# Softmax denominators of a causal latent attention: added over key blocks on VectorE, then summed by one set of products per chunk of heads

## The chip, the cores and the metric

The kernel runs on one core of one Trainium2 chip. The metric is device time in microseconds (us) of one execution. The kernel before took 2323.1 us in the median of three runs (2315.94 to 2333.15).

Names used below: PE is TensorE (matrix products), PEld its weight loads, DVE is VectorE, ACT is ScalarE, POOL is GpSimd, SP is the engine that issues most transfers.

## The reference, cut to what matters

The kernel computes a network of two layers on `x` of shape (2, 1024, 128): latent attention, a spiking feed-forward, a state-space block, linear attention, head attention and mixtures of experts. The change touches only the first block, for batch 0:

```python
q = einsum('bld,dhk->blhk', x_bld, Wq)
latent = einsum('bld,dc->blc', x_bld, Wkv_down)
k = einsum('blc,chk->blhk', latent, Wk_up)
v = einsum('blc,chk->blhk', latent, Wv_up)
attn = einsum('bqhd,bkhd->bhqk', q, k) / sqrt(64)
attn = softmax(where(causal mask, attn, -big), axis=-1)
y = einsum('bhqk,bkhd->bqhd', attn, v)
out = einsum('bqhd,hdo->bqo', y, Wout)
```

There are 16 heads, 1024 queries and keys, and a latent of 32 numbers. All is float32, but for the small bfloat16 operands named below.

## The kernel before, in words

`LatentAttention` folds the key weights into the queries, so that a score is a product over the 32 latent numbers, and uses the latent itself as the values. The 16 heads are four chunks `c` of four heads `j`. The four heads of a chunk lie in the four groups of 32 partitions.

`attend(b, ...)` does one batch, in two halves of 512 queries. Half 0 has 4 key blocks of 128 keys, half 1 has 8. A unit of work is one pair (chunk, key block), so half 0 has 16 units and half 1 has 32. In a unit `exponentials` (L282 to L301) does:

- L282: four float32 products, one for each head, that give the scores with keys on partitions. Each takes 32 rows of the array and all 128 columns. The shapes in the profile read 32\*128.
- L291: four bfloat16 products that add the negative row maximum of each query. They use the same 32 rows.
- L301: two ACT instructions that take the exponential of two heads each, from the PSUM tile `a0_st` (3 buffers of two heads) to the SBUF tile `a0_pT` (6 buffers of two heads).
- L304: on a diagonal block, where keys and queries meet, POOL sets what the causal mask forbids to zero, 128x256 elements for each pair of heads. All 4 blocks of half 0 and the last 4 of half 1 are diagonal. On these the width falls from 512 queries to 384, 256 and 128.

Then `weigh` (L320 to L336) does, one unit later:

- L320: four products of the exponentials with the latent, one for each head. Each takes all 128 rows and 32 columns of the array (128\*32 in the profile). They accumulate over the key blocks in the PSUM tile `a0_oT`, which has one buffer.
- L328: four products of the same exponentials with columns of ones, into the PSUM tile `a0_dT`. They accumulate the denominators over all chunks and key blocks of the half. Also 128\*32.
- L336: after the last key block of a chunk, DVE copies `a0_oT` to `a0_oU`.

The steps run one unit ahead: the scores of unit k+1 are issued ahead of the weighing of unit k. At the end of a half DVE takes the reciprocal of `a0_dT` (L348), PE spreads it over the heads (L352), DVE multiplies (L353), PE applies the output weights (L358) and DVE adds to the residual (L362).

Batch 0 runs by itself (`drain(latent.attend(0, ...))`, L1217), and a list scheduler decides the order of instructions on each engine there. Batch 1 runs in an order written by hand: `weave(space[0].loop(work, bank), attend, 1.75)` takes 1.75 steps of `attend(1)` for each step of the state-space loop (L637 to L639: two products and one scan on DVE for each step), then drains the rest. A step is what lies between two `yield`s.

In the profile a float32 product counts twice, since it is done in two passes: four products are x8. A bfloat16 product counts once. A short name such as `a_pT` stands for `a0_pT`.

Of the kernel before, what the change touches and what calls it, by code (L numbers as in the profile page):

```python
# [9 lines left out]
F32 = mybir.dt.float32  # L10
# [9 lines left out]
P = 128  # L20
# [67 lines left out]
def drain(steps):  # L88
    for _ in steps:
        pass  # L90
# [20 lines left out]
class LatentAttention:  # L111
# [3 lines left out]
    C, J, LD = 4, 4, 32  # L115
# [146 lines left out]
        nc.vector.tensor_copy(self.nmT[b], pt.rearrange("p a b -> p (a b)"))  # L262
        yield

    def attend(self, b, work, ps, ps_o):
        g, nc, C, J = self.g, self.g.nc, self.C, self.J
        qT, latT, lat, nmT = self.qT[b], self.latT[b], self.lat[b], self.nmT[b]
        for half in range(2):
            kbs = list(range(4 * half + 4))
            dT = ps_o.tile([P, 512], F32, name="a0_dT")  # L270
            oU = work.tile([P, C, 512], F32, name="a0_oU")
            oTs = {}

            def exponentials(c, kb):

                off = max(kb * P - half * 512, 0)
                q0 = half * 512 + off
                n = 512 - off
                ss = [ps.tile([P, 2, 512], F32, name="a0_st") for _ in range(2)]
                for j in range(J):  # L280
                    quad = slice(32 * j, 32 * j + 32)
                    nc.tensor.matmul(  # L282
                        ss[j // 2][:, j % 2, off:],
                        latT[quad, bass.ts(kb, P)],
                        qT[quad, c, q0 : q0 + n],
                        start=True,
                        stop=False,
                    )
                for j in range(J):
                    quad = slice(32 * j, 32 * j + 32)  # L290
                    nc.tensor.matmul(  # L291
                        ss[j // 2][:, j % 2, off:],
                        self.addm[quad, c, :],
                        nmT[quad, q0 : q0 + n],
                        start=False,
                        stop=True,
                    )
                pTs = []
                for s in ss:
                    pT = work.tile([P, 2, 512], F32, name="a0_pT", bufs=6)  # L300
                    nc.scalar.activation(pT[:, :, off:], s[:, :, off:], AF.Exp)  # L301
                    if kb * P >= half * 512:
                        diag = pT[:, :, off : off + P]
                        nc.gpsimd.affine_select(  # L304
                            out=diag,
                            in_=diag,
                            pattern=[[0, 2], [1, P]],
                            compare_op=ALU.is_ge,
                            fill=0.0,
                            base=0,  # L310
                            channel_multiplier=-1,
                        )
                    pTs.append(pT)
                return pTs, off

            def weigh(c, kb, pTs, off):
                if kb == 0:
                    oTs[c] = ps_o.tile([P, 512], F32, name="a0_oT")
                for j in range(J):
                    nc.tensor.matmul(  # L320
                        oTs[c][32 * j : 32 * j + 32, off:],
                        lat[:, kb, :],
                        pTs[j // 2][:, j % 2, off:],
                        start=(kb == 0),
                        stop=(kb == kbs[-1]),
                    )
                for j in range(J):
                    nc.tensor.matmul(  # L328
                        dT[32 * j : 32 * j + 32, off:],
                        self.ones[:, c, :],  # L330
                        pTs[j // 2][:, j % 2, off:],
                        start=(c == 0 and kb == 0),
                        stop=(c == C - 1 and kb == kbs[-1]),
                    )
                if kb == kbs[-1]:
                    nc.vector.tensor_copy(oU[:, c, :], oTs.pop(c))  # L336

            units = [(c, kb) for c in range(C) for kb in kbs]
            held = {}
            for step in range(len(units) + 1):  # L340
                if step < len(units):
                    held[step] = exponentials(*units[step])
                if step >= 1:
                    weigh(*units[step - 1], *held.pop(step - 1))
                yield

            rec = work.tile([P, 512], F32, name="a0_rec")
            nc.vector.reciprocal(rec, dT)  # L348
            yield
            for c in range(C):  # L350
                rr = ps.tile([P, 2, 512], F32, name="a0_st")
                nc.tensor.matmul(rr[:, 0, :], self.pick[:, c, :], rec, start=True, stop=True)  # L352
                nc.vector.tensor_mul(oU[:, c, :], oU[:, c, :], rr[:, 0, :])  # L353
            yield
            for i in range(4):
                pf = ps.tile([P, 2, 512], F32, name="a0_st")
                for c in range(C):
                    nc.tensor.matmul(  # L358
                        pf[:, 0, :D], oU[:, c, bass.ts(i, P)], self.wvo[:, c, :], start=(c == 0), stop=(c == C - 1)
                    )  # L360
                xt = g.x[:, b * TPB + 4 * half + i, :]
                nc.vector.tensor_add(xt, xt, pf[:, 0, :D])  # L362
            yield
# [832 lines left out]
def first_layer(g, w, open_experts, load_expert):  # L1196
# [3 lines left out]
    def pool(stack, name, bufs, **kw):  # L1200
        return stack.enter_context(tc.tile_pool(name=name, bufs=bufs, **kw))
# [7 lines left out]
    latent = LatentAttention(g, w, pool(latents, "a0_keep", 1, **right))  # L1209
    own = pool(latents, "a0_batch1", 1, **right)  # L1210
    with ExitStack() as es:
        latent.project([pool(es, "a0_batch0", 1), own])
        with tc.tile_pool(name="a0_seq", bufs=1) as seq, tc.tile_pool(name="a0_ps_a", bufs=2, space=PSUM) as ps:
            drain(latent.row_maxima(0, seq, ps, 4))
        work = pool(es, "a0_work", 2)
        ps, ps_o = pool(es, "a0_ps_b", 3, space=PSUM), pool(es, "a0_ps_o", 1, space=PSUM)
        drain(latent.attend(0, work, ps, ps_o))  # L1217

    bank = banks(spaces, "bank", 2)
    shared = StateConstants(g, w, pool(spaces, "s_one", 1))  # L1220
# [25 lines left out]
    with tc.manual_schedule(engines=ALL):  # L1246
        with (
            tc.tile_pool(name="a0_seq", bufs=1, **right) as aseq,
            tc.tile_pool(name="a0_ps_a", bufs=3, space=PSUM, **right) as ps,
        ):  # L1250
            maxima = latent.row_maxima(1, aseq, ps, 2)
            weave(into_space(0, bank), maxima, 1.25)
            drain(maxima)
        work = pool(latents, "a0_work", 1, **right)
        ps, ps_o = pool(latents, "a0_ps_b", 2, space=PSUM, **right), pool(latents, "a0_ps_o", 1, space=PSUM, **right)
        attend = latent.attend(1, work, ps, ps_o)
        with tc.tile_pool(name="s_work", bufs=1, reuse_waits="tile") as work:
            weave(space[0].loop(work, bank), attend, 1.75)
        drain(attend)
        latents.close()  # L1260
        open_experts()
        with ExitStack() as es:
            bank0, bank1 = banks(es, "bank0", 3, **right), banks(es, "bank1", 3, **right)
            side = into_space(1, bank1, **right)
            weave(out_of_space(0, bank0, load_experts()), side, 1.2)
            drain(side)
        ework = pool(ends, "e_work", 2, **right)
        ps_e, ps_o = pool(ends, "e_ps", 2, space=PSUM, **right), pool(ends, "e_ps_o", 1, space=PSUM, **right)
        experts = expert_steps(g, w, [0, 1], ework, ps_e, ps_o)
        with tc.tile_pool(name="s_work", bufs=1, reuse_waits="tile") as work:  # L1270
            weave(space[1].loop(work, bank), experts, 1.4)
        spaces.close()
        with ends, ExitStack() as es:
            weave(out_of_space(1, banks(es, "bank", 3)), experts, 0.6)
            drain(experts)
# [3 lines left out]
def kernel(ctx: ExitStack, tc: tile.TileContext, d: dict, out: bass.AP):  # L1279
# [30 lines left out]
    def load_expert(e):  # L1310
        for name in ("Wg", "Wu"):
            nc.sync.dma_start(out=w[name][:, e, :], in_=d[name][e])
        nc.sync.dma_start(out=w["Wd"][:, e], in_=d["Wd"][e].rearrange("(c p) o -> p c o", p=P))

    first_layer(g, w, open_experts, load_expert)
    layer0.close()
    experts_ffn(g, w, [2])
# [70 lines left out]
```

## Time and profile before

| what | value |
|---|---|
| median of three runs | 2323.1 us |
| the profiled execution: its time / its span | 2328.53 us / 2326.8 us |
| products of batch 0, half 0 (147.87 to 198.51 us) | 50.64 us |
| its end: reciprocal to the next scores | 12.30 us |
| products of batch 0, half 1 (210.81 to 305.49 us) | 94.68 us |
| its end | 14.04 us |
| PE busy / DVE busy / ACT busy in the products of half 1 | 92.72 / 3.63 / 53.50 us |
| state-space loop with batch 1 (486.9 to 703 us) | 216.10 us |
| PE busy / DVE busy over the whole span | 87% / 70% |

The stages lie one after the other on the time axis of the trace. A busy PE in this profile is not a PE at its peak: a product that fills a quarter of the array counts as busy just as one that fills it.

The order of the built program can be listed engine by engine. On PE it is the order in which the trace shows the products, with one freedom that the prediction describes.

### The profile page before, as it was taken

What the parts mean: (1) busy time and instruction counts of PE and PEld (TensorE: products, weight loads), DVE (VectorE), ACT (ScalarE), POOL (GpSimd) and SP (SyncE); (2) the same over time, 40 slices, a digit from 0 to 9 for tenths busy, and PEclk for the clock granted to TensorE, in tenths of its full rate; (3) what the DMA queues carried; (4) which work ended last, traced back from release to release, by engine and by line L of the source; (5) the groups of instructions that cost most, each with busy time, mean ns of one, the idle gap of its engine ahead of it and who ended that gap; (6) DMA issues with size and microseconds to landing.
All of it is one profiled execution on the core that took longest, in us unless ns stands there. A gap on an engine that the chain in (4) does not pass through costs nothing. (4 is left out here: it accounts for less than half of the span.)

```text
span 2326.8 us, 36810 instructions
## 1 busy us (share of the span) xinstructions
PE 2015.9 (87%) x15152; PEld 1184.5 (51%) x15152; DVE 1629.0 (70%) x1988; ACT 1183.5 (51%) x1486; POOL 854.9 (37%) x460
## 2 busy tenths in 40 slices
PE   7779988887987748789698799999977999999999
PEld 4323344323334313235345577677755777777754
DVE  5851047788974659993423699899978999999732
ACT  1014521353643458764322576777735777777632
POOL 0001100033320000000102277878788787877700
PEclk9789997878998879899799899999989999999999
DMA  3000000076732067640000266566556665665500
GB/s 86 1 1 1 2 1 1 18 190 152 185 93 89 4 159 184 162 106 0 1 1 0 64 153 157 145 152 157 146 150 152 157 155 155 153 162 146 137 5 5
DMA packets 72647, 220.19 MB, mean 95 GB/s; under 512 B 9056, under 2 KB 19744, under 8 KB 72352
## 3 DMA queue, kind: packets, MB, share of 16 engines
q1 hardware_dynamic: 53584, 149.40, 21.5%
q0 software_dynamic: 18432, 67.12, 15.3%
q8 instruction: 119, 1.95, 0.3%
q10 hardware_dynamic: 464, 1.33, 0.3%
q14 instruction: 48, 0.39, 0.1%
HBM read 78.35 MB, written 5.24 MB: 36 GB/s over the span
## 5 line engine op out<-in xcount | busy, mean ns | idle before, releaser
L1075 POOL TENSOR_TENSOR h_a<-h_e,h_r 128x2048 f32<-128x2048 f32 x128 | 581.4, 4542 | 130.4 <-PE h_po L1081 93.9
L1041 DVE TENSOR_REDUCE h_m<-h_s 128x128 f32<-128x2048 f32 x128 | 293.2, 2291 | 73.2 <-PE h_s L1030 73.1
L1065 PE MATMUL h_pd<-h_e,ident 128*128 128x128 f32 x2048 | 267.4, 285 | 43.4 <-DMA h_e<-h_e 29.6
L1050 ACT ACTIVATE h_e<-h_e 128x1024 f32<-128x1024 f32 x256 | 256.5, 1049 | 89.6 <-DVE h_e L1047 71.4
L1047 DVE TENSOR_TENSOR h_e<-h_s,h_m 128x2048 f32<-128x2048 f32 x128 | 292.6, 2286 | 3.4 <-DVE h_m L1041 1.7
L1065 PEld LDWEIGHTS h_pd<-h_e,ident 128*128 128x128 f32 x2048 | 244.6, 196 | 87.3 <-DVE x_res L914 41.5
L304 POOL TENSOR_SCALAR_AFFINE_SELECT a_pT<-a_pT 128x256 f32<-128x256 f32 x128 | 97.2, 775 | 431.4 <-ACT a_pT L301 430.5
L301 ACT ACTIVATE a_pT<-a_st 128x1024 f32<-128x1024 f32 (+1 forms) x192 | 145.1, 808 | 139.1 <-PE a_st L291 137.0
L886 ACT ACT_TABLE_LOAD x105 | 134.7, 1283 | 150.5 <-PE e_pgu L879 150.3
L806 DVE TENSOR_TENSOR e_h<-e_sg,e_pu 128x512 f32<-128x512 f32 x128 | 87.0, 686 | 176.5 <-PE e_pu L802 151.2
L243 DVE TENSOR_REDUCE a_nm<-a_s 128x2 f32<-128x1024 f32 (+7 forms) x144 | 168.4, 1218 | 48.5 <-PE a_s L234 24.2
L804 ACT ACTIVATE e_sg<-e_pg 128x512 f32<-128x512 f32 x128 | 76.0, 596 | 192.5 <-PE e_pg L801 192.3
L825 PE MATMUL e_po<-e_h,Wd 128*128 128x512 f32 x256 | 139.4, 630 | 39.4 <-DVE e_h L806 39.3
L225 PE MATMUL a_s<-a_latT,a_qT 32*128 32x512 f32 (+3 forms) x768 | 128.7, 650 | 49.4 <-DVE a_nm L243 47.6
L905 PEld LDWEIGHTS h_pd<-Wd,e_h 128*128 128x128 f32 x1024 | 125.5, 191 | 90.1 <-DVE e_h L894 76.8
L1030 PE MATMUL h_s<-h_qz,h_kT 32*128 32x512 f32 x1024 | 148.5, 649 | 19.5 <-DVE h_e L1047 13.9
L879 PE MATMUL e_pgu<-e_uT,Wg 128*128 128x256 f32 x512 | 154.1, 383 | 4.0 <-ACT h_qz L994 2.1
L905 PE MATMUL h_pd<-Wd,e_h 128*128 128x128 f32 x1024 | 149.1, 287 | 5.9 <-DVE e_h L894 3.7
L879 PE MATMUL e_pgu<-e_uT,Wu 128*128 128x256 f32 x512 | 152.3, 379 | 0.0
L1060 POOL DMA_DIRECT2D h_e<-h_e x128 | 113.6, 887 | 104.0 <-DVE h_m L1041 48.8
L638 DVE TENSOR_TENSOR_SCAN s_h<-s_a,s_h 128x1024 f32<-128x1024 f32 x64 | 147.4, 2303 | 5.9 <-ACT s_a L606 1.7
L801 PE MATMUL e_pg<-e_uT,Wg 128*128 128x512 f32 x256 | 141.9, 638 | 2.1 <-ACT e_uT L794 2.1
(246 smaller groups left out, 3191.6 us busy)
## 6 DMA issues: line engine op xcount, KB each, us to landing
h_e<-h_e SPq DMA_DIRECT2D x128, 512.0 KB, 4.0
h_e<-h_e POOLq DMA_DIRECT2D x128, 512.0 KB, 4.6
s_a<-s_steps SPq DMA_DIRECT2D x64, 512.0 KB, 4.8
s_h<-s_steps SPq DMA_DIRECT2D x64, 512.0 KB, 6.3
s_steps<-s_delta SPq DMA_DIRECT2D x4, 512.0 KB, 2.6
s_steps<-s_dtx SPq DMA_DIRECT2D x4, 512.0 KB, 3.4
Wg<-in_Wg_dram SPq DMA_DIRECT2D x8, 256.0 KB, 6.0
Wu<-in_Wu_dram SPq DMA_DIRECT2D x8, 256.0 KB, 5.9
```

The lines of the kernel that those rows point to most:

```text
L243: nc.vector.tensor_reduce(nm[:, half, i, h : h + together], s[:, :, :n], AX.X, ALU.max, negate=True)
L301: nc.scalar.activation(pT[:, :, off:], s[:, :, off:], AF.Exp)
L638: nc.vector.tensor_tensor_scan(h, a, h, 0.0, ALU.mult, ALU.add)
L801: nc.tensor.matmul(pg, w["Wg"][:, e, f], opened[n], start=True, stop=True)
L879: nc.tensor.matmul(pgu[:, k, :], w[name][:, e, f], uT, start=True, stop=True)
L905: nc.tensor.matmul(po[:, t, :], h[:, bass.ts(t, P)], self.w["Wd"][:, e, fc, :], start=(k == 0), stop=(k == 1))
L1030: nc.tensor.matmul(s[:, j, :].rearrange("p (k q) -> p k q", k=K), kTs[b][quad, bass.ts(kb, P)], qzs[b][quad, :, bass.ts(qb, P)], start=Tru ...
L1041: nc.vector.tensor_reduce(m, heads.rearrange("p h q -> p q h"), AX.X, ALU.max)
L1047: nc.vector.tensor_sub(e, heads, m.unsqueeze(1).to_broadcast([P, H, P]))
L1050: nc.scalar.activation(eh, eh, AF.Exp, scale=scale)
L1065: nc.tensor.matmul(pd, g.ident, e2[:, k, :], start=(k == 0), stop=(k == 7))
L1075: nc.gpsimd.tensor_mul(a, e, r.unsqueeze(1).to_broadcast([P, H, P]))
```

## The change

For batch 0 alone (`added=True`):

- The exponentials of key block 0 of a chunk go to two new tiles, `a0_sum0` and `a0_sum1` (two buffers each), in place of `a0_pT`.
- The products with ones are no longer issued for each unit. For every key block after the first, DVE adds the exponentials to the sum tiles, two instructions for each unit (L347 of the changed kernel).
- One set of four products with ones for each chunk (L324 of the changed kernel) sums the tiles over the keys. It is issued one step after the weighing of the chunk's last block.
- The loop over steps has one step more, for both batches: `range(len(units) + 2)`. For batch 1 the added step holds no work, but it is a `yield`, so that `attend(1)` has 64 of them in place of 62.

```diff
-    def attend(self, b, work, ps, ps_o):
+    def attend(self, b, work, ps, ps_o, added=False):
...
-                for s in ss:
-                    pT = work.tile([P, 2, 512], F32, name="a0_pT", bufs=6)
+                for k, s in enumerate(ss):
+                    if added and kb == 0:
+                        pT = work.tile([P, 2, 512], F32, name=f"a0_sum{k}")
+                        total[c, k] = pT
+                    else:
+                        pT = work.tile([P, 2, 512], F32, name="a0_pT", bufs=6)
...
+            def denominators(c, pTs, off, first, last):
+                for j in range(J):
+                    nc.tensor.matmul(
+                        dT[32 * j : 32 * j + 32, off:],
+                        self.ones[:, c, :],
+                        pTs[j // 2][:, j % 2, off:],
+                        start=first,
+                        stop=last,
+                    )
...
-                for j in range(J):
-                    nc.tensor.matmul(
-                        dT[32 * j : 32 * j + 32, off:],
-                        self.ones[:, c, :],
-                        pTs[j // 2][:, j % 2, off:],
-                        start=(c == 0 and kb == 0),
-                        stop=(c == C - 1 and kb == kbs[-1]),
-                    )
+                if not added:
+                    denominators(c, pTs, off, c == 0 and kb == 0, c == C - 1 and kb == kbs[-1])
+                elif kb > 0:
+                    for k, pT in enumerate(pTs):
+                        nc.vector.tensor_add(total[c, k][:, :, off:], total[c, k][:, :, off:], pT[:, :, off:])
...
-            for step in range(len(units) + 1):
+            for step in range(len(units) + 2):
                 if step < len(units):
                     held[step] = exponentials(*units[step])
-                if step >= 1:
+                if 1 <= step <= len(units):
                     weigh(*units[step - 1], *held.pop(step - 1))
+                if added and step >= 2 and units[step - 2][1] == kbs[-1]:
+                    c = units[step - 2][0]
+                    denominators(c, [total.pop((c, k)) for k in range(2)], 0, c == 0, c == C - 1)
                 yield
...
-        drain(latent.attend(0, work, ps, ps_o))
+        drain(latent.attend(0, work, ps, ps_o, added=True))
```

The scheduler of batch 0 then builds another order on PE. Below is that order for half 0, from the weighing of block 1 of the second chunk to that of the third chunk, in both programs. S is scores (L282), M the row maximum (L291), W weighing (L320), D ones (L328), with the width behind the letter; a and b are the two pairs of heads, 1 and 2 a single head of pair a; a bar stands where PE goes from products of the 32\*128 shape to the 128\*32 shape or back.

```
before: W384ab D384ab | S128ab M | W256ab D256ab | S512a M S512b M | W128ab D128ab | S384ab M |
        D512a | S256a | W512ab D512b | M S256b M | W384ab ...
after:  W384a | S128(1) | W384b | S128(2) M S128b M | W256a | S512(1) | W256b | S512(2) M S512b M |
        W128a | S384(1) | W128b | S384(2) M | D512a | S384b M | D512b | S256a M | W512ab | S256b M | W384a ...
```

And one chunk of half 1, from the weighing of its block 1 to that of the next chunk:

```
before: W512ab D512ab | S512 M | W512ab D512ab | S512 M | W512ab D512ab | S384 M | W512ab D512ab | S256 M |
        W384ab D384ab | S128 M | W256ab D256ab | S512 M | W128ab D128ab | S512 M | D512ab | S512(1) |
        W512ab | S512(2) M S512b M | W512ab ...
after:  W512ab | S512 M | W512ab | S512 M | W512ab | S384 M | W512a | S256(1) | W512b | S256(2) M S256b M |
        W384ab | S128 M | W256a | S512(1) | W256b | S512(2) M S512b M | W128a | S512(1) | W128b |
        S512(2) M | D512a | S512b M | D512b | S512a | W512ab | S512b M | W512ab ...
```

More of the change, by code (lines that the diff above doesn't have):

```diff
@@ L271, in attend @@
             oU = work.tile([P, C, 512], F32, name="a0_oU")
-            oTs = {}
+            oTs, total = {}, {}
             def exponentials(c, kb):
```

## The prediction

> **What bounds the kernel now.** I read the stages in the windows view first, because the change touches only the attention of batch 0, then the timeline of one unit, then a unit whose groups are broken, then the waits.
>
> ```profile
> core 0: us, PE busy (x) PEld busy (x) DVE busy (x) ACT busy (x) POOL busy (x), PEclk, DMA share, GB/s
> 147.87:198.51 50.64, 49.01 (x448) 18.15 (x448) 2.68 (x5) 23.43 (x34) 12.81 (x32) 0.93 0.01 1
> 210.81:305.49 94.68, 92.72 (x897) 29.13 (x896) 3.63 (x9) 53.50 (x67) 13.51 (x33) 0.98 0.01 1
> ```
>
> In both product stages PE is busy almost throughout, ACT about half of the time, DVE hardly at all. So PE bounds them, and what PE sheds could count. How much a product is worth has to be read from starts:
>
> ```profile
> 222.56 1.15 PE L282 MATMUL a_st<-a_qT,a_latT 32*128 32x512 f32 x8
> 223.52 0.40 PE L291 MATMUL a_st<-a_nmT,a_addm 32*128 32x512 bf16 x4
> 223.85 1.06 PE L320 MATMUL a_oT<-a_pT,a_lat 128*32 128x512 f32 x8
> 224.00 1.94 ACT L301 ACTIVATE a_pT<-a_st 128x1024 f32<-128x1024 f32 x2 [1.20 <-PE a_st L291]
> 224.73 1.04 PE L328 MATMUL a_dT<-a_pT,a_ones 128*32 128x512 f32 x8
> 225.70 1.14 PE L282 MATMUL a_st<-a_qT,a_latT 32*128 32x512 f32 x8
> ```
>
> Four products of one kind, one for each head, run side by side and take one slot: 0.96 us for the scores, 0.33 for the row maximum, 0.88 for the weighing, 0.97 for the products with ones with the turn back to scores. The next rows show what a slot costs that is not full:
>
> ```profile
> 179.60 1.05 PE L328 MATMUL a_dT<-a_pT,a_ones 128*32 128x512 f32 x4
> 180.58 0.70 PE L282 MATMUL a_st<-a_qT,a_latT 32*128 32x256 f32 x4
> 181.21 1.06 PE L320 MATMUL a_oT<-a_pT,a_lat 128*32 128x512 f32 x8
> ...
> 240.20 1.12 PE L282 MATMUL a_st<-a_qT,a_latT 32*128 32x512 f32 x2
> 241.25 1.06 PE L320 MATMUL a_oT<-a_pT,a_lat 128*32 128x512 f32 x8
> 242.25 0.69 PE L282 MATMUL a_st<-a_qT,a_latT 32*128 32x512 f32 x1
> ```
>
> One head's score (x2) takes 1.05 us to the next start, two heads' ones (x4) 0.98: as much as four. And the two shapes do not overlap. So the price is set by how often PE changes between 32\*128 and 128\*32, not by how many products there are. From such rows I take, for widths 512, 384, 256 and 128: scores 0.965, 0.75, 0.54, 0.32; row maximum 0.325, 0.27, 0.22, 0.17; weighing or ones 0.89, 0.67, 0.46, 0.24; 0.09 more where PE turns from 128\*32 to 32\*128, or back straight from scores. (Groups of a and b that stand in one stretch between two bars count once.)
>
> ```profile
> DVE a_oU L336 <- PE a_oT L320: 138.9, 8, 25.7
> L637 DVE TENSOR_TENSOR s_h<-s_h,s_Bx x64: 1161/1219/1425, 486.9 to 1035.7; 128x1024 f32<-128x1024 f32 x64
> L304 POOL TENSOR_SCALAR_AFFINE_SELECT a_pT<-a_pT x128: 401/407/2387, 152.8 to 674.3; 128x256 f32<-128x256 f32 x128
> ```
>
> The first row, of the waits of 150 to 345 us, says that DVE sat idle 138.9 us waiting for PE: room for the added work. The second prices an addition of the new kind, both operands in SBUF. The third is for the contention below.
>
> **Part by part.**
>
> *Products with ones.* 192 products become 32: 160 leave, which looks like 40 slots. By the rebuilt order it is otherwise. Taken out, they leave the weighing waiting for ACT or POOL, and the scheduler fills that with the next scores, one head at a time. Stretches of one shape rise from 108 to 156 (half 0 40 to 68, half 1 68 to 94).
>
> Half 0, one chunk in the order that the change lists. Before, ten stretches: 1.43 + 0.49 + 1.01 + 1.29 + 0.57 + 1.02 + 0.98 + 0.63 + 1.87 + 0.76 = 10.05 us; the trace has 10.66 for it (173.15 to 183.81), the rest being a wait for ACT. After, 18 stretches by row of the list: W384a to S128b M 0.76 + 0.41 + 0.76 + 0.49 = 2.41; W256a to S512b M 0.55 + 1.06 + 0.55 + 1.29 = 3.43 (rounded parts); W128a to S384(2) M 0.33 + 0.84 + 0.33 + 1.02 = 2.51; D512a to S256a M 0.98 + 1.02 + 0.98 + 0.76 = 3.73; W512ab and S256b M 1.74. Sum 13.8 us: 3.1 us more, with fewer products.
>
> Half 1, one chunk. Before: 2 x (1.865 + 1.29) + 2.885 + 2.625 + 1.915 + 2.295 + 1.855 + 4.295 = 22.18 us; trace 22.83 (220.70 to 243.53). After: 2 x 2.27 + 2.00 + 3.34 + 1.25 + 3.43 + 3.00 + 4.30 + 2.27 = 24.1 us. Here 0.89 us is saved in each of the three units that stay whole, and more is lost in five broken places.
>
> Summed over the whole order, half 0 goes from 43.0 to 50.2 us, half 1 from 87.5 to 89.9.
>
> *Waits.* In a whole unit of half 1, ACT takes 2 x 1.0 us and the period falls to 2.27, so pair b's weighing waits for ACT where ones used to stand: I take 2.39 (from 224.00 + 1.94 to the next), 0.12 for each of three. On the diagonal 0.7 a chunk for selects that DVE stretches (next item). So 24.1 + 0.4 + 0.7 = 25.2 us a chunk. Half 0 keeps its start waits, less one cold D512.
>
> *Additions on DVE.* 80 instructions. Width 2x512 1.22 us (L637), 2x256 0.69 (the copies of 128x512), 2x384 between them, 0.95 as an estimate; 2x128 0.42, between 0.29 (L362, 128x128) and 0.69. Half 0: 8 x (0.95 + 0.69 + 0.42) = 16.5 us; half 1: 8 x (4 x 1.22 + 0.95 + 0.69 + 0.42) = 55.5. All beside PE: 72 of the 138.9 idle us. A whole unit wants 2.45 us of DVE against 2.39 of PE, a lag that block 0 (no addition) repays: 14 us of DVE a chunk against 25. Queued behind an addition is only the copy L336, which frees `a0_oT`; between the last weighing of a chunk and the first of the next stand two ones stretches and two score stretches, 3.7 us, against 0.42 x 2 + 0.69. Cost 0; without that cover, at most 0.84 x 8 = 7 us.
>
> *Selects on POOL.* 32 diagonal units, 0.41 us each alone. Next to DVE instructions with two SBUF inputs (batch 1 runs beside L637 and L639) they stretch: the mean of the 128 is 775 ns, so batch 1's 64 average 2 x 0.775 − 0.41 = 1.14, up to 2.39. Bounds here: 0 to 1 us for each unit. I take 0 in half 0, where a one-head score stretch stands between a select and its weighing, and the 0.7 above in half 1; these are the nearest, since DVE is busy a third to a half of the time here.
>
> *Ends of the halves.* The last set of ones waits for DVE's last addition and takes 0.98 in place of 0.24: +1.5 in half 0, +0.4 in half 1 where more of it is covered. Half 0: start −2.0 (the first W384 at 160.47 before, at about 158.5 after, one cold D512 less), nothing for the first chunk (12.7 by its stretches, 12.68 in the trace), 3.14 for each of the next two, tail +1.5: reciprocal at about 204.4 against 198.51, +5.9 (rounded). By sums, 50.2 + 4.85 start waits + 1.6 tail = 56.6 against 50.64, the same. Half 1: start −0.8, three chunks x (25.2 − 22.83) = +7.0, tail +0.4: +6.6.
>
> *ACT and memory.* ACT does the same exponentials, into other tiles; the two buffers of each sum tile come free a chunk ahead. DMA: SP's order is unchanged, nothing is queued past anything. Cost 0.
>
> *The added step of batch 1.* `attend(1)` has 64 yields in place of 62, of which the 35 steps of the loop take 61.25. In the middle PE, with 1.75 x 3.3 us of units a step, stays the slower one beside DVE's 4.8 us a step: 0 (bounds −2 and +2). At its end the order on DVE changes: the scan of the last step (679.12 to 683.9 in the trace, between reciprocal and L353) now stands before the reciprocal, and its results feed PE while DVE is at the residual. From 675.25 to the last L664 the trace has 27.7 us; with the reordered rows I get 24.0: −3.7 (bounds −6 and +1).
>
> Sum: +5.9 + 6.6 − 3.7 = **+8.8 us** on the profiled 2328.53, 2337. That run lies 5.4 above the median of three, so 2332 against 2323.1: +0.4%. What a measurement here can tell from no change is about 1%.
>
> *A rule against the trace.* The four scores start within 0.03 us of each other at 222.56 although the built order of many units is S of pair a, M of a, S of b, M of b, and M starts at 223.52 only: later instructions pass an earlier one that waits. The Trainium skill, "TensorE: Matmul & The Clock Gate", Part 3 ("Packing small matmuls"), has matmuls strictly in program order. By it each unit with M ahead of S b would pay a second score slot; such units rise from 30 to 44 of 48, 8.4 us more, and the sum would be +17. The measured starts decide; the sum above does not use the rule.
>
> **Rivals.**
>
> 1. *The removed products are paid in full* (faster). It needs broken groups to overlap with the other shape. A chunk then loses its ones slots, less one set of 0.98: 2.26 − 0.98 in half 0, 5.82 − 0.98 in half 1, four each: −24.5 us, and with −3.7 at the end of batch 1, 2295. Against it: 240.20 to 241.25, one head alone at full price.
> 2. *Selects or additions hold PE* (slower). If each of the 32 diagonal units waited as long as batch 1's selects stretch at the typical worst, 1.38 against 0.41, it is +31 on top: 2363. It takes over 1% from about 14 such units on. For it: 2.39 us seen. Against: DVE here is far less busy than with batch 1.
> 3. *The granted clock falls* (slower), because PE's half-filled stretches count as less: 0.98 in half 1 against 0.86 and 0.76 in the ends of the halves. some 100 us of half 1 at 0.81 (the mean of those two) in place of 0.98 are about +20: 2352. For it: half 0 stands at 0.93 with its waits. Against: PE does not pause more.
> 4. *The broken groups cost nothing* because waits for ACT in the old order go at the same time: only the end of batch 1 and small gains remain, about −4: 2319.
>
> **How the numbers follow.** Forecast 0.73 (its own range 2321 to 2344: −2 to +21 on the median, from the bounds of selects, the batch-1 end and the split chunks); rival 1 0.05, rival 2 0.12, rival 3 0.04, rival 4 0.06. Faster by over 1% is rival 1, 0.05. Slower by over 1% (above 2346) is rivals 2 and 3 and 0.03 of the forecast's upper end, 0.19; the rest 0.76. The range 2312 to 2353 takes in rivals 3 and 4 and leaves out 1 and 2, 0.17, and a little at the edges.
>
> **What would show it.** Product stages of about 56.5 and 101 us; middle chunks of 13.8 and 25.2 us between the same weighings; one-head and two-head stretches at full price; additions of 1.22 us beside PE, no wait of PE on DVE but at the ends; L304 near 0.41 in half 0 and stretched in half 1; a clock still at 0.93 and 0.98; the end of the loop some 4 us earlier against its start. Wrong if a one-head stretch is cheaper than 1 us beside the other shape, if PE waits for POOL by more than 1 us a chunk, or if the clock falls.

## The result, and the profile after

The changed kernel took 2340.4 us in the median of 20 executions (2325.0 to 2375.1), the kernel before 2322.1 (2312.0 to 2334.6, also 20). The ratio is 1.0062, with a 95% interval of 1.0040 to 1.0084: about 14 us slower, 0.6%. Ratios, here and below, leave out executions over 1.5% above the fastest of their kernel, here the four longest of the 20 (2361 and up); the medians keep them, and by the medians the change is 18 us slower. The forecast was 2332, and +8.8 us.

The profiled execution took 2328.1 us, with a span of 2326.4: as long as that of the kernel before (2326.8). So the first lesson is that this one pair of profiles does not show the loss. The windows view of the changed kernel, same columns as before:

```profile
core 0: us, PE busy (x) PEld busy (x) DVE busy (x) ACT busy (x) POOL busy (x), PEclk, DMA share, GB/s
142.56:198.18 55.62, 53.62 (x352) 17.65 (x352) 19.52 (x29) 23.68 (x34) 14.77 (x32) 0.97 0.00 1
211.73:308.48 96.75, 93.80 (x673) 27.52 (x672) 59.90 (x66) 53.84 (x67) 22.57 (x33) 1.00 0.00 1
```

Half 0 now has 352 records of products in place of 448, and half 1 has 673 in place of 897. Yet they take 55.6 us (+5.0) and 96.75 us (+2.1). PE is busy throughout as before. DVE has gone from 2.7 and 3.6 us to 19.5 and 59.9.

| stage (profiled pair) | before | after | difference |
|---|---|---|---|
| up to the first score of batch 0 (untouched) | 147.87 | 142.56 | −5.3 |
| products of half 0 | 50.64 | 55.62 | +5.0 |
| reciprocal to next scores | 12.30 | 13.55 | +1.3 |
| products of half 1 | 94.68 | 96.75 | +2.1 |
| its end | 14.04 | 13.44 | −0.6 |
| state-space loop with batch 1, start of the first scan (the instruction behind the first L637) to the end of batch 1's last addition to the residual | 214.74 | 209.32 | −5.4 |
| all that follows, and the stage ahead of the scan | | | +2.6 |

The sum is −0.4. The first line goes with a clock difference in a stage that both kernels share: 0.86 before (0 to 147.87 us) and 0.93 after (0 to 142.56 us), with PE busy 104.0 and 96.8 us.

The timeline of the changed kernel, first a whole unit of half 1, then a broken group of half 0:

```profile
222.45 1.15 PE L284 MATMUL a_st<-a_qT,a_latT 32*128 32x512 f32 x8
223.41 0.40 PE L293 MATMUL a_st<-a_nmT,a_addm 32*128 32x512 bf16 x4
223.75 1.06 PE L336 MATMUL a_oT<-a_pT,a_lat 128*32 128x512 f32 x8
224.74 1.09 PE L284 MATMUL a_st<-a_qT,a_latT 32*128 32x384 f32 x8
...
167.09 0.63 PE L336 MATMUL a_oT<-a_pT,a_lat 128*32 128x256 f32 x4
167.65 1.12 PE L284 MATMUL a_st<-a_qT,a_latT 32*128 32x512 f32 x2
168.70 0.63 PE L336 MATMUL a_oT<-a_pT,a_lat 128*32 128x256 f32 x4
```

A stretch is what PE does between two changes of shape; a thin one holds products of one or two heads in place of four. From 222.45 to 224.74 a unit without ones takes 2.29 us, where the kernel before needed 3.14 (222.56 to 225.70). But at 167.65 one head's score takes 1.05 us to the next start, between two weighings of two heads each. Such places ate the saving.

The waits of 150 to 350 us and two rows by line:

```profile
DVE a_sum L347 <- PE a_oT L336: 45.3, 8, 7.2
DVE a_oU L349 <- PE a_oT L336: 19.5, 8, 3.2
```

```profile
L347 DVE TENSOR_TENSOR a_sum<-a_sum,a_pT x80: 409/958/1476, 149.7 to 306.5; 128x1024 f32<-128x1024 f32 x32, 128x768 f32<-128x768 f32 x16, 128x512 f32<-128x512 f32 x16, 128x256 f32<-128x256 f32 x16
```

```profile
L310 POOL TENSOR_SCALAR_AFFINE_SELECT a_pT<-a_pT x120: 401/710/2387, 149.1 to 676.8; 128x256 f32<-128x256 f32 x120
```

DVE still waits for PE for 65 us, so it is not the bound. The 80 additions lie between 0.41 and 1.48 us, by width. The median of the selects rose from 407 to 710 ns. That row has batch 1's in it, which were stretched before; of batch 0's, the 32 of half 0 took 14.77 us in all, 0.46 each, and the 32 of half 1 21.87 us, 0.68 each, where each had taken 0.41.

### The profile page after: what moved, and what is told of

Read it like the earlier page. It is cut to its first block, busy times and chain, and to the rows that moved or that the text cites. A ratio compares the mean times of both kernels' runs of the same rounds, so it can differ in the third digit from the quotient of the medians.

```text
span 2326.4 us, 36321 instructions
## 1 busy us (share of the span) xinstructions
PE 2011.6 (86%) x14832; PEld 1173.1 (50%) x14832; DVE 1701.8 (73%) x2068; ACT 1183.8 (51%) x1486; POOL 866.5 (37%) x460
## 3 DMA queue, kind: packets, MB, share of 16 engines
q1 hardware_dynamic: 53584, 149.40, 21.6%
## 5 line engine op out<-in xcount | busy, mean ns | idle before, releaser
L310 POOL TENSOR_SCALAR_AFFINE_SELECT a_pT<-a_pT 128x256 f32<-128x256 f32 x120 | 104.8, 892 | 314.4 <-ACT a_pT L307 313.7
L307 ACT ACTIVATE a_pT<-a_st 128x1024 f32<-128x1024 f32 (+3 forms) x176 | 130.4, 789 | 124.2 <-PE a_st L293 122.0
L225 PE MATMUL a_s<-a_latT,a_qT 32*128 32x512 f32 (+3 forms) x768 | 122.9, 615 | 51.0 <-DVE a_nm L243 49.3
L654 DVE TENSOR_TENSOR_SCAN s_h<-s_a,s_h 128x1024 f32<-128x1024 f32 x64 | 147.0, 2297 | 5.5 <-ACT s_a L622 1.2
```

The lines of the kernel that those rows point to most:

```text
L654: nc.vector.tensor_tensor_scan(h, a, h, 0.0, ALU.mult, ALU.add)
```

## The experiments

The theories. **Groups**: the scheduler's new order breaks the groups of four heads, and thin stretches cost as much as whole ones. **Contention**: DVE's additions stretch the selects on POOL, and PE waits. **Clock**: the thin order changes what clock PE is granted. In all tables, ratios are to the kernel before on the same chip, with 95% intervals.

### The changed kernel again, three profiles in all

No edit: a second series of 12 executions, then one single execution more, each with a profile.

> The changed kernel once more, nothing edited, to see what of its time belongs to the stages and what to the granted clock. Theory (broken groups of four heads): the products of half 0 take 55.6 us again and those of half 1 96.8 us, whatever the whole time, the end of batch 1's loop is again 4 to 7 us earlier, and the time is 2330 to 2345. Rival (the granted clock): where the whole time is above 2340, a stage that the change does not touch, or half 1, shows a lower granted clock than the 0.97 and 1.00 of the first profile and is longer for it, by about 1.9 us for each 0.001 of the mean clock.

> The changed kernel a third time, one look. Theory (the clock in half 0 makes the spread): the time of this execution follows the stretch that half 0 spends at half clock: about 2328 where that is under 8 us, half a microsecond more for each further microsecond at half clock, all other stages within 3 us of the first two profiles. Rival: the time differs by stages elsewhere.

Measured: 1.0078 (1.0050 to 1.0106), median 2346.9 of 12 executions (2328 to 2381). The profile taken there is of an execution at that median (2346.6), with a span of 2344.9. Half 0 took 71.3 us in place of 55.6, half 1 98.4. The stages behind half 1 agree with the first profile within 2 us. Half 0 in the windows view:

```profile
142.30:145.70 3.40, 3.40 (x16) 1.51 (x18) 0.00 (x0) 0.82 (x1) 0.00 (x0) 0.52 0.00 0
145.70:149.00 3.30, 2.11 (x14) 0.54 (x10) 0.00 (x0) 3.29 (x5) 0.93 (x3) 1.00 0.00 0
149.00:182.70 33.70, 33.70 (x130) 9.48 (x128) 8.30 (x11) 7.64 (x13) 5.38 (x13) 0.50 0.00 0
182.70:213.56 30.86, 29.93 (x198) 9.54 (x196) 11.39 (x17) 11.92 (x18) 7.78 (x18) 0.99 0.01 1
```

The third line matters most. For 33.7 us PE is busy all the time, 33.70 of 33.70, and its granted clock is 0.50. In the first profile half 0 was at half clock only for its first 3.5 us:

```profile
142.56:146.06 3.50, 3.50 (x16) 1.52 (x18) 0.00 (x0) 0.92 (x1) 0.00 (x0) 0.50 0.00 0
146.06:198.18 52.12, 50.12 (x338) 16.13 (x334) 19.52 (x29) 22.76 (x34) 14.77 (x32) 1.00 0.00 1
```

The third profiled execution took 2341.7 us with 16.7 us at half clock in half 0, which lasted 61.0 us. Half 0 thus grows by 0.4 to 0.5 us for each microsecond at half clock (15.6 us for 33.6 more, 5.4 for 13.2 more). The whole time of the third was longer than the rule of its expectation says (about 2332); 5 us of it lie behind 1061 us, in code that the change does not touch.

The theory that half 0 takes 55.6 us whatever the whole time fell: the other stages repeat, but the clock of half 0 does not. The rival had the clock right and its place wrong.

### The added step alone

```diff
-            for step in range(len(units) + 1):
+            for step in range(len(units) + (1 if b == 0 else 2)):
...
```

> The kernel before with one part of the change: the loop of batch 1 has one empty step more in each half, and batch 0 is as before. Theory: the end of the state-space loop with batch 1 comes 4 to 7 us earlier, all else stays, so 2316 to 2319 beside about 2322. Rival (the shift is an accident of the two profiles): no change, within 2 us.

Measured: 0.9988 (0.9966 to 1.0010), 2322.3 against 2327.1. The loop with batch 1 took 208.2 us. It took 214.7, 211.4 and 211.2 in the three profiles of kernels without the added step, and 208.2 to 209.9 in the eleven with it: means 212.4 and 209.1, so −3.3 us (−2.2 without the 214.7), where 4 to 7 were expected. The timed difference points the same way, and its interval takes in no change.

### Whole groups: the order by hand, with and without the change

```diff
-        drain(latent.attend(0, work, ps, ps_o, added=True))
+        with tc.manual_schedule(engines=ALL):
+            drain(latent.attend(0, work, ps, ps_o, added=True))
```

> The change, with batch 0 in the order in which the code issues it, so that the four heads of a group stand together again; same instructions. Theory (broken groups): a chunk is then at least 7.1 us in half 0 and 16.2 in half 1 by the prices of whole groups, with waits for ACT perhaps 9.5 and 18, against 13.9 and 24.7 in the changed kernel: 40 to 45 us less, about 2295. Rival (selects on POOL and additions on DVE hold PE): the waits stay, half 1 keeps 24 us a chunk, and the time stays at 2330 to 2340. Second rival (an order without filling leaves PE waiting for ACT as much as the broken groups cost): 2325 to 2345.

The same edit on the kernel before:

> The kernel before, with batch 0 in the order in which the code issues it. Tells whether the order alone does it. Theory (broken groups): whole groups cost 8.4 us a chunk in half 0 and 21.1 in half 1, against 10.7 and 22.8 in the trace: at most 16 us less, with waits for ACT about 10 less, 2312. So of the gain of the run above some 30 us belong to the products taken out. Rival: the order by hand alone gives as much as the run above, and the products with ones were not worth anything.

| | ratio | chunk, half 0 | chunk, half 1 |
|---|---|---|---|
| before, scheduler's order | 1 | 10.66 and 10.28 | 22.8 |
| changed, scheduler's order | 1.0062, 1.0078 | 13.85 | 24.6 |
| before, by hand | 0.9951 (0.9929 to 0.9974) | 9.42 | 21.6 |
| changed, by hand | 0.9917 (0.9883 to 0.9950) | 9.21 | 19.4 |

(Chunks are from the weighing of block 1 to that of the next chunk, at full clock.) Same instructions, other order: the changed kernel went from 0.8% slower to 0.8% faster, 2310.0 against 2346.9, both timed on one chip. (About 2295 had been expected.) That settles that the order costs it the gain. The fourth line against the third is what the removed products are worth by the chunks where groups stay whole: 0.2 us a chunk in half 0 and 2.2 in half 1, some 10 us in all. The windows of half 1, first the kernel before by hand, then the changed kernel by hand:

```profile
200.70:293.36 92.66, 88.88 (x898) 28.02 (x896) 5.28 (x12) 53.60 (x67) 15.19 (x33) 0.98 0.01 1
200.51:282.66 82.15, 76.39 (x673) 23.70 (x672) 61.95 (x72) 53.62 (x67) 25.86 (x33) 1.00 0.01 1
```

The whole times, 2315.4 and 2310.0, do not separate the two: their intervals overlap. I had expected 30 us; PE shed 12.5 us of busy time in half 1, and stands idle 5.8 us there in place of 3.8.

### Additions without their time

In the order by hand; most of the denominators is left out.

```diff
-                        nc.vector.tensor_add(total[c, k][:, :, off:], total[c, k][:, :, off:], pT[:, :, off:])
+                        nc.vector.tensor_add(total[c, k][:, :, 508:], total[c, k][:, :, 508:], pT[:, :, 508:])
```

> The change in the order by hand, with DVE's additions cut from the whole width to the last 4 columns: same instructions, same waits, same order on every engine, almost no DVE time. Leaves out most of the denominators. Theory (in the order by hand the additions cost PE time through the selects on POOL): selects go back to 0.41 us, the waits of PE for POOL nearly go, and a chunk of half 1 falls from 19.4 to about 17.5 us: 8 us less than the order by hand, about 2302. Rival (the additions are free): same stages within 1 us and the same time as the order by hand, 2310.

The row of the selects, first with the full additions, then with the small ones:

```profile
L310 POOL TENSOR_SCALAR_AFFINE_SELECT a_pT<-a_pT x120: 401/881/2387, 151.3 to 651.1; 128x256 f32<-128x256 f32 x120
```

```profile
L310 POOL TENSOR_SCALAR_AFFINE_SELECT a_pT<-a_pT x120: 401/407/2386, 149.6 to 642.6; 128x256 f32<-128x256 f32 x120
```

The median went back from 881 to 407 ns, PE's weight loads waited 9.9 us for POOL in place of 18.7 (140 to 310 us), and a chunk fell from 9.21 to 8.75 us and from 19.4 to 18.3: 6 us in all. So the additions are not free in this order, and the wait that shrinks with them is that for POOL. (8 us had been expected.) The time was 0.9852 (0.9816 to 0.9888), 2295.3. Of the 15 us below the order by hand, 10 lie behind 1028 us in the two profiles, in code that the edit does not touch; I do not count them.

### Whole groups where the clock is low

```diff
-        drain(latent.attend(0, work, ps, ps_o, added=True))
+        steps = latent.attend(0, work, ps, ps_o, added=True)
+        with tc.manual_schedule(engines=ALL):
+            for _ in range(5):
+                next(steps)
+        drain(steps)
```

> The changed kernel, with the first chunk of half 0 alone in the order of the code, so that whole groups of four heads stand there while PE's granted clock is still at half; the rest in the scheduler's order. Theory (the long executions are those in which thin groups do not raise the clock in half 0): the clock rises within 15 us of the first scores as in both orders by hand, no execution above about 2345, median about 2328. Rival (the spread has another place): the times reach above 2360 as often as those of the changed kernel, median 2340 or more.

Measured: 0.9986 (0.9962 to 1.0009), median 2324.4, and the longest of 12 executions 2337.1, where the changed kernel went up to 2381. The clock rose 11.6 us after the first scores. The first chunk is shorter too (9.05 in place of 12.69 us) and the next two (12.58 in place of 13.85), about 6 us; the remaining 16 of the 22 us to the changed kernel's median of 2346.9 would fit the clock. Half 0 took 49.8 us in its profile. In that profile the clock fell once later, at the thin end of a chunk of half 1; half 1 had 0.92 in the mean and took 104.6 us. The stretch ahead of the fall and the one behind it:

```profile
278.50:281.90 3.40, 3.40 (x22) 1.00 (x17) 0.69 (x1) 1.94 (x2) 0.00 (x0) 0.99 0.00 0
281.90:298.90 17.00, 17.00 (x59) 3.46 (x62) 4.72 (x4) 4.16 (x5) 0.00 (x0) 0.50 0.00 1
```

PE is busy throughout both. So here the clock fell with no pause of PE ahead of it, among products of one and two heads, and stayed down for 17.0 us.

### A dense stretch ahead of half 0, in both kernels

```diff
+        if b == 0:
+            warm = ps.tile([P, 4, 512], F32, name="a0_warm", tag="a0_s")
+            for k in range(5):
+                nc.tensor.matmul(warm[:, k % 4, :], self.g.ident, qT[:, k % 4, 0:512], start=True, stop=True)
         pt = ps.tile([P, TPB, P], BF16, name="a0_mt", tag="a0_s")
```

> The changed kernel with five float32 products over the whole array, whose result is not used, in the pause of PE ahead of half 0; everything behind it in the same order. Theory (the clock): the pause no longer lowers the clock, half 0 starts at full clock and takes about 51 us in place of 55.6 to 71.3, the executions lie close together, 2322 to 2335, median about 2326. Rival (the spread has another place): 2340 as before, or more by the products' own time.

> The kernel before with the same five products over the whole array ahead of half 0. Theory (what keeps the clock at half is the changed kernel's order of thin groups, not the products ahead): the clock may fall at the first wait for ACT as it did there, but comes back within 15 us, half 0 takes 45 to 52 us and the time stays within 8 us of the kernel before. Rival (the products ahead themselves bring the long stretch at half clock): half 0 above 70 us and 2350 or more, as in the changed kernel with these products.

This was the sharpest contrast, and my expectation for the first of them was wrong. The changed kernel with these products took 1.0182 (1.0133 to 1.0231), 2374.8. It did start at full clock, lost it at the first wait for ACT, and did not get it back for the rest of half 0:

```profile
142.28:146.70 4.42, 2.79 (x22) 1.31 (x24) 0.00 (x0) 3.00 (x3) 0.41 (x1) 0.96 0.00 0
146.70:235.00 88.30, 88.30 (x322) 24.00 (x318) 18.27 (x27) 20.27 (x32) 13.98 (x31) 0.50 0.00 1
```

Half 0 took 94.6 us, its chunks 23.6 to 25.7. The kernel before with the same products took 0.9993 (0.9971 to 1.0015). It lost the clock at the same kind of wait, and had it back 3.2 us later:

```profile
143.50:148.70 5.20, 3.56 (x26) 1.45 (x28) 0.00 (x0) 3.77 (x4) 0.82 (x2) 0.98 0.00 0
148.70:151.90 3.20, 3.20 (x10) 0.56 (x8) 0.00 (x0) 0.85 (x2) 0.82 (x2) 0.50 0.02 5
151.90:193.03 41.13, 40.69 (x416) 15.42 (x416) 2.68 (x4) 18.80 (x29) 11.24 (x28) 1.00 0.01 1
```

So the products ahead are not the cause by themselves. Nor are the instructions of the change: in the order by hand they ran at full clock behind the same products (next section). What is left is the scheduler's new order. In it PE can stay at half clock for long: 11.8 us without a pause in the third profile of the changed kernel, 33.7 in the second, 88.3 here.

### By hand, with a dense stretch and with two units of distance

The five products ahead of the order by hand:

> The change in the order by hand with the five products ahead of it. Theory (the clock): half 0 starts at full clock, some 5 us less than the order by hand, about 2303. Rival: the order by hand raises the clock in time anyway, 2308 to 2312.

Measured: 0.9905 (0.9877 to 0.9933), 2307.3. Half 0 ran at 1.00 throughout and took 39.5 us in place of 42.8. Its chunks stayed at 9.2 us. The whole time does not tell it from the order by hand alone (0.9917).

Then the weighing two units behind the scores, and that with the products ahead:

```diff
+            lag = 2 if added else 1
...
-                if 1 <= step <= len(units):
-                    weigh(*units[step - 1], *held.pop(step - 1))
+                if lag <= step < len(units) + lag:
+                    weigh(*units[step - lag], *held.pop(step - lag))
...
```

> The change in the order by hand, with the weighing two units behind the scores in place of one, so that no weighing waits for its own select. Theory (what is left above the prices of whole groups is waiting for ACT, POOL and DVE): a chunk comes near 8 us in half 0 and 17.5 in half 1, against about 9 and 19.4 in the order by hand: some 12 us less than it, about 2297. Rival (the third buffer pair of scores, freed by ACT, is what PE waits for, whatever the weighing does): within 4 us of the order by hand, 2308.

> The order by hand with the weighing two units behind, and the five products over the whole array ahead of half 0. Theory (whole groups keep or soon regain the clock): half 0 starts at full clock, at most one dip of 3 to 4 us at the first waits for ACT, and falls from 41.9 to about 36 us: about 2296. Rival (the long waits for ACT at the start lower the clock and it stays low for 10 us or more): half 0 at 40 us or above, 2300 to 2303.

Measured: 0.9899 (0.9872 to 0.9925), 2301.9 (2297 expected), chunks 8.17 and 18.06 us; and with the products ahead 0.9893 (0.9871 to 0.9915), 2301.0, half 0 39.3 in place of 41.9. Both have the lowest times here of kernels that compute all of it, about 25 us below the kernel before, though the intervals do not separate them from the order by hand with the products ahead. The distance was worth 1.0 and 1.3 us a chunk. The products ahead add nothing that can be measured in the whole time (2296 had been expected): half 0 lost the clock 4 us in and ran 6.8 us at half clock anyway.

## Why the prediction was right, and where it was not

The direction and the range held. The forecast's mechanism, broken groups, is shown by the order alone turning the sign. That the number came as near as it did is partly luck: by the stages, the terms that the forecast had counted gave less than it said, and one that it had put at nothing, the clock of half 0, added to them. Its terms, on the profiled pair:

| term | forecast | measured |
|---|---|---|
| half 0, to the first W384 | −2.0 | −3.2 (9.40 against 12.60) |
| first chunk | 0 | 0.0 (12.69 against 12.68) |
| next two chunks | +6.3 | +6.8 (13.85 each) |
| tail | +1.5 | +1.4 |
| half 1, start | −0.8 | −2.7 |
| three chunks | +7.0 | +5.4 (24.6 each) |
| tail | +0.4 | −0.7 |
| added step of batch 1 | −3.7 | −3.3 by the means of 14 profiles |

Two sums of the forecast are off by 0.1 us: its terms of half 0 add up to 5.8, not 5.9, and three times 25.2 − 22.83 is 7.1, not 7.0. Nothing rests on it.

*Counting groups* was right to 0.1 us a chunk in half 0: 13.85 against 13.8.

*The rule of strict program order* is not borne out. By the estimate in the prediction, "TensorE: Matmul & The Clock Gate", Part 3, would have put another 8.4 us on the units with M ahead of S b. The chunks measured agree with the sum without it, and M of pair a still starts behind the scores of both pairs (223.41 after 222.45, by 0.96 us, the time of one slot).

*The selects* were mis-sized. I took 0.7 us a chunk of half 1 for selects stretched by DVE; 24.6 us measured against 24.1 by groups alone leaves 0.5 for selects and lag together, where I had 1.1. In the scheduler's order other work stands between a select and its weighing. In the order by hand the same contention costs 1.1 us a chunk of half 1, so the effect is real, and rival 2 (slower by 31 us) had the right mechanism with too high a price.

*The start of half 1* looks better than forecast because the kernel before ran 3 of its first 10 us at half clock in its profile and the changed kernel did not. In the second profile of the changed kernel, which has such a dip, the start took 8.86 us against 9.89: −1.0, near the forecast.

*The clock in half 0* is the step that failed: "Half 0 keeps its start waits, less one cold D512", with the clock taken as in the profile of before. A falling clock was one of the prediction's own signs of being wrong. Rival 3 (chance 0.04) had the clock fall, but put it in half 1 and against it that "PE does not pause more". It was half 0, and pauses were not the point: its reason, that half-filled stretches count as less, fits the runs better than its place and its price do. The terms above sum to +3.7 on the profiled pair, and to +5.4 with the start of half 1 from the second profile. The executions measured are 14 to 18 us slower. The rest, 9 to 14 us, is what 20 to 31 more microseconds at half clock than in the first profile would cost at 0.46 us each. The first profile of the changed kernel had 3.5 us of it in half 0, the other two 16.7 and 37.1; the four profiles of kernels that issue the ones unit by unit had 3.4 to 11.4. That share is worked out, not measured in the timed executions, since those have no record of the stage.

They do have a record of the mean clock of the whole span, and their times follow it: over the 20 executions of the result the correlation is −0.97. In the second series the changed kernel's executions had 0.931 in the mean and those of the kernel before 0.937. A straight line with one slope for both (1.8 us for each 0.001) leaves 12 us (9 to 16) between them at equal mean clock, out of 23 us between their mean times. That is more than the +5.4 of the terms. The mean does not say in which stage the clock was low, so how the loss divides between the broken groups and the clock stays open. That the clock of half 0 has a share rests on the three profiles, on the first chunk by hand, which took the long executions away, and on the dense stretch, which made them all long.

What exactly raises the clock stays open. In the second profile it rose at about 183 us, in a stretch of the same kind as that which had not raised it before. Nothing was tried that varies only how full a stretch is.

## What to carry to other kernels

Where products that fill part of the array run side by side, count stretches between changes of shape, not products: taking products out can make a list scheduler (which fills a wait with whatever is ready next) break the groups that made the others cheap. Compare the built orders before believing a gain, and if the order is what was lost, write it by hand. When a kernel's times spread more than before, take several profiles and line up the granted clock by stage: one profile can be the lucky one.

## What the runs showed of the hardware that was not expected

A PE that the profile shows busy without a gap can stay at half clock: 33.7 us and 88.3 us at 0.50 with 33.70 and 88.30 us busy, when its stretches hold one or two heads. It can even fall to half clock with no pause ahead: 3.40 of 3.40 us busy at 0.99, then 17.00 of 17.00 at 0.50 (the profile of the first chunk by hand). In the same kind of order it can also keep 1.00 (the 52.1 us of the first profile, with 50.12 busy). The Trainium skill, "TensorE: Matmul & The Clock Gate", Part 1, has the full clock come after one busy window of about 3.4 us. The kernel before agrees where its groups are whole (3.2 us at half clock after its wait), and whole groups by hand took at most 7.1 us of unbroken work; the changed kernel does not agree, and the measurement decides: busy time as the profile shows it is not what is counted.
